# A greedy order's table of positions: rows of their own for the first and the last image, and new numbers in every row

## The chip, the cores and the metric

The kernel runs on one core of one Trainium2 chip. The metric is the device time of one execution in microseconds; of the kernel before, three runs gave 2142.4, 2146.23 and 2150.11, median 2146.23.

## The reference

The input x is 16 images of 256 channels and 56 x 56 points, float32. Two blocks follow each other, each added to its input:

```python
x = x + conv(_gn(x))        # _gn: group norm, 32 groups of 8 channels
x = x + attention(_gn(x))
```

`conv` takes the sign of its input, convolves it with weights of which only the sign and one scale per channel count (3 x 3, four groups of 64 channels, dilations 1, 3 and 5), puts each of the three results through a leaky rectifier with its own slope, sums them and normalizes over the channels. `attention` makes q, k and v of 64 channels (8 heads of 8), forms for each point the nine neighbours' scores out of q times k (a fixed and a learned depthwise part, folded into one small matrix here), takes the softmax over the nine, sums the nine values and projects back to 256 channels.

## The kernel before, in words

**Tiles.** Each image is cut into two strips (u = 0 and 1), each of four pieces of seven rows; a tile of a strip is 128 partitions x 784 points (two halves of 392). One image takes these stages, for each strip u:

- `stats`, `norm0`, `sign`: load x by channel group (`load_half`, L468), sums on ACT (L489), group norm's shift, sign into the padded bf16 image `sgn` (L514), of which there is one per channel group, and an exchange of border rows (L526, L527).
- `conv{u}`: twelve steps, channel group g by dilation d (`conv`, L554): 36 matmuls (L564) into one PSUM buffer, then ACT (L583, for d = 0, and L596) and DVE (L590, for d = 1 and 2, and L602) sum the three results in a buffer `ct`.
- `load{u}` loads x once more into `xt` (L1148). `mean{u}`, `var{u}`, `root{u}`, `scale{u}` normalize the four ct of the strip (`channel_norm`, L641: matmuls L613 and L631, DVE L660 and L689, ACT L667) and add them to xt (L703, on POOL), with the squares of the sum on ACT (L710).
- `fold`, once per image after both strips: the second group norm is folded into the weights of q, k and v (`fold`, L722; POOL L732, PE L755).
- `qkv{u}`: 16 matmuls each for q, k and v (L794), evicted by ACT (L812).
- `prod{u}`: nine products of q and a shifted k (L850); `term{u}`: ten groups of matmuls that sum them into scores (L872), in two PSUM buffers for the whole strip; `soft{u}`: transposes and the softmax (L886 to L908, on DVE, ACT and POOL).
- `value{u}`: ten groups of matmuls (L922), each evicted by a DVE product with a shifted v (L934) into a buffer `m` and summed (L948); `proj{u}`: four projections (L968) that DVE adds to xt (L979); then the store (L989).

**Buffers.** PSUM is four buffers of two banks (`ps`). There are seven `ct`, three `xh`, three `xt`, three `p` and three `m`. A strip holds its xt from the load to the store.

**What sets the order.** The kernel schedules by hand. Every step is registered with `plan.at(stage, b, i)` (L186) and an operation on an engine with a cost in us, the buffers it needs and what it reads and writes. `Plan.emit` (L223) then simulates the five engines with those costs and writes each engine's instructions in the order that it finds. In each round it takes, per engine, the operation that can start first; among those whose starts lie within AHEAD it takes the one of the lowest position, `2 * b + ORDER[stage][i]`. So 2 in the table is one image, a step at −20 goes before nearly everything, and one at 95 goes when nothing else can. Buffers of xh, xt, ct, p and m are given out in program order alone: a step that must open such a buffer waits for the earlier ones, whatever its position. HOP (0.25 us) is the planner's price of a dependency between engines.

`either` (L413) leaves products, the sum of the values and the addition to xt to POOL or DVE: DVE may take one only when it would end it more than LEAN (61.83 us) before POOL, or, for the products and sums of the last image, when LAST (−32.05) is added to its end in place of LEAN.

**The table.** ORDER has, for each stage, a row for the first image (name with `^`), one for the images between (plain) and one for the last (`$`). Before the change the three rows of a stage hold the same numbers:

```python
"term0^": (-17.28, 5.04, -6.13, -15.6, 8.43, 19.29, 31.53, 24.74, -8.75, 0.82),
"term0": (-17.28, 5.04, -6.13, -15.6, 8.43, 19.29, 31.53, 24.74, -8.75, 0.82),
"term0$": (-17.28, 5.04, -6.13, -15.6, 8.43, 19.29, 31.53, 24.74, -8.75, 0.82),
```

The order of the program (before the planner) is: weights and the first image's signs, then for each image b both strips' convolutions and channel norms, the signs of image b + 1, the fold of b, q, k and v of both strips, scores and values of strip 0, then of strip 1.

Of the kernel before, what the change touches and what calls it, by code (L numbers as in the profile page):

```python
# [68 lines left out]
class Op:  # L69
# [6 lines left out]


ORDER = {
    "first^": (24.59,),
    "second^": (30.61,),  # L80
    "start^": (-0.44, 12.01, 8.32, -11.9),
    "weights^": (16.57, 0.74, 15.54, 8.13, -15.35, 9.81),
    "stats": (-23.02, -11.03, 24.25, 43.57),
    "stats$": (-23.02, -11.03, 24.25, 43.57),
    "norm0": (-20.32,),
    "norm0$": (-20.32,),
    "sign": (-8.81, 4.11, 13.27, 36.85),
    "sign$": (-8.81, 4.11, 13.27, 36.85),
    "conv0^": (-17.27, 2.29, 28.55, -15.99, 8.45, 8.78, -5.4, 6.78, 31.53, -11.69, 14.22, 14.25),
    "conv0": (-17.27, 2.29, 28.55, -15.99, 8.45, 8.78, -5.4, 6.78, 31.53, -11.69, 14.22, 14.25),  # L90
    "conv0$": (-17.27, 2.29, 28.55, -15.99, 8.45, 8.78, -5.4, 6.78, 31.53, -11.69, 14.22, 14.25),
    "conv1^": (7.4, 12.95, 95.96, 12.79, 1.59, 12.9, 4.7, 39.18, 55.69, -8.93, 9.19, 30.54),
    "conv1": (7.4, 12.95, 95.96, 12.79, 1.59, 12.9, 4.7, 39.18, 55.69, -8.93, 9.19, 30.54),
    "conv1$": (7.4, 12.95, 95.96, 12.79, 1.59, 12.9, 4.7, 39.18, 55.69, -8.93, 9.19, 30.54),
    "load0^": (95.98,),
    "load0": (95.98,),
    "load0$": (95.98,),
    "load1^": (5.24,),
    "load1": (5.24,),
    "load1$": (5.24,),  # L100
    "mean0^": (8.83,),
    "mean0": (8.83,),
    "mean0$": (8.83,),
    "mean1^": (29.44,),
    "mean1": (29.44,),
    "mean1$": (29.44,),
    "var0^": (8.78, 11.01, 15.97, 29.02),
    "var0": (8.78, 11.01, 15.97, 29.02),
    "var0$": (8.78, 11.01, 15.97, 29.02),
    "var1^": (-9.01, 16.63, 18.58, 16.63),  # L110
    "var1": (-9.01, 16.63, 18.58, 16.63),
    "var1$": (-9.01, 16.63, 18.58, 16.63),
    "root0^": (-10.53,),
    "root0": (-10.53,),
    "root0$": (-10.53,),
    "root1^": (-17.05,),
    "root1": (-17.05,),
    "root1$": (-17.05,),
    "scale0^": (15.67, 15.06, -3, 40.43),
    "scale0": (15.67, 15.06, -3, 40.43),  # L120
    "scale0$": (15.67, 15.06, -3, 40.43),
    "scale1^": (-16.84, 17.23, 8.22, 8.83),
    "scale1": (-16.84, 17.23, 8.22, 8.83),
    "scale1$": (-16.84, 17.23, 8.22, 8.83),
    "fold^": (-12.89,),
    "fold": (-12.89,),
    "fold$": (-12.89,),
    "qkv0^": (6.66, -12.93, 15),
    "qkv0": (6.66, -12.93, 15),
    "qkv0$": (6.66, -12.93, 15),  # L130
    "qkv1^": (8.11, -17.4, 96.15),
    "qkv1": (8.11, -17.4, 96.15),
    "qkv1$": (8.11, -17.4, 96.15),
    "prod0^": (9.09, 30.51, 9.14, -13.48, 29.6, 14.43, 17.51, -16.64, -13.31),
    "prod0": (9.09, 30.51, 9.14, -13.48, 29.6, 14.43, 17.51, -16.64, -13.31),
    "prod0$": (9.09, 30.51, 9.14, -13.48, 29.6, 14.43, 17.51, -16.64, -13.31),
    "prod1^": (-14.1, 12.39, 13.44, 5.73, 7.96, 13.89, -14.32, -16.31, -9.81),
    "prod1": (-14.1, 12.39, 13.44, 5.73, 7.96, 13.89, -14.32, -16.31, -9.81),
    "prod1$": (-14.1, 12.39, 13.44, 5.73, 7.96, 13.89, -14.32, -16.31, -9.81),
    "term0^": (-17.28, 5.04, -6.13, -15.6, 8.43, 19.29, 31.53, 24.74, -8.75, 0.82),  # L140
    "term0": (-17.28, 5.04, -6.13, -15.6, 8.43, 19.29, 31.53, 24.74, -8.75, 0.82),
    "term0$": (-17.28, 5.04, -6.13, -15.6, 8.43, 19.29, 31.53, 24.74, -8.75, 0.82),
    "term1^": (-16.84, 29.94, 29.34, 11.93, 6.96, 8.07, -9.43, 13.66, 9.05, 6.97),
    "term1": (-16.84, 29.94, 29.34, 11.93, 6.96, 8.07, -9.43, 13.66, 9.05, 6.97),
    "term1$": (-16.84, 29.94, 29.34, 11.93, 6.96, 8.07, -9.43, 13.66, 9.05, 6.97),
    "soft0^": (-14.93,),
    "soft0": (-14.93,),
    "soft0$": (-14.93,),
    "soft1^": (7.31,),
    "soft1": (7.31,),  # L150
    "soft1$": (7.31,),
    "value0^": (-13.35, -23.05, -1.34, 4.34, -6.07, 9.15, -16.95, -21.09, -15.61, 39.19),
    "value0": (-13.35, -23.05, -1.34, 4.34, -6.07, 9.15, -16.95, -21.09, -15.61, 39.19),
    "value0$": (-13.35, -23.05, -1.34, 4.34, -6.07, 9.15, -16.95, -21.09, -15.61, 39.19),
    "value1^": (-19.04, 4.84, -9.61, -12.73, 6.92, 7.45, 12.47, 8.08, 28.72, 39.07),
    "value1": (-19.04, 4.84, -9.61, -12.73, 6.92, 7.45, 12.47, 8.08, 28.72, 39.07),
    "value1$": (-19.04, 4.84, -9.61, -12.73, 6.92, 7.45, 12.47, 8.08, 28.72, 39.07),
    "proj0^": (-0.81, 7.32, -11.88, -8.96),
    "proj0": (-0.81, 7.32, -11.88, -8.96),
    "proj0$": (-0.81, 7.32, -11.88, -8.96),  # L160
    "proj1^": (15.51, -16.48, -1.88, 6.47),
    "proj1": (15.51, -16.48, -1.88, 6.47),
    "proj1$": (15.51, -16.48, -1.88, 6.47),
}


class Plan:
# [5 lines left out]


    HOP = 0.25
    LEAN = 61.83
    LAST = -32.05
    AHEAD = 0.29

    def __init__(self, kinds, last):  # L180
        self.kinds, self.ops, self.wrote, self.read = kinds, [], {}, {}
# [10 lines left out]
    def op(self, eng, cost, emit, r=(), w=(), port=False, hold=(), late=0.0, other=None, lean=None):  # L192
# [6 lines left out]
        o = Op(engines, self.prio, emit, bufs, port, late)  # L199
        o.lean = self.LEAN if lean is None else lean  # L200
        for b in bufs:
# [21 lines left out]
    def emit(self):  # L223
# [4 lines left out]
        while ready:  # L228
            short, best = set(), {}
            for x in ready:  # L230
# [18 lines left out]
                for e, cost in o.engines:  # L249
# [3 lines left out]
                    elif start + cost + o.lean > done:  # L253
                        continue
                    if e not in best or start < best[e][0] - self.AHEAD:
                        best[e] = (start, x, e, cost)
# [35 lines left out]
def preact_conv_attention(  # L292
# [120 lines left out]
    def either(costs, f, r, w, b):  # L413


        engines = {"POOL": nc.gpsimd, "DVE": nc.vector}
        op("POOL", costs[0], lambda e: f(engines[e]), r, w, port=True, other=("DVE", costs[1]), lean=Plan.LAST if b == NB - 1 else None)

# [879 lines left out]
```

## Time and profile before

| what | value |
|---|---|
| runs, median (lowest to highest) | 2146.23 us (2142.4 to 2150.11) |
| the profiled execution | 2151.76 us, span 2150.0 us |
| TensorE clock granted, mean | 0.953 of full |
| instructions | 70814 |
| HBM read, written | 154.91 MB, 51.38 MB |
| first weight scaling of the fold (L732), image 0 | 155.8 us |
| the same, image 15 | 2049.1 us |

How to read what follows: an engine's busy time is that of its own instructions; a group "out<-in" names what an instruction writes and reads; "<-X" at the end of a line names what ended the idle time ahead of it. A count "x36" of L564 is one convolution step. PE is TensorE, DVE VectorE, ACT ScalarE, POOL GpSimd, and SP issues the transfers. The scaling of the weights at L732 marks the fold, so the distance from one to the next is the period of the images.

### The profile page before, as it was taken

The page shows a single profiled execution, that of the slowest core. Times are in us where ns is not written, and L with a number is a line of the kernel's source. Part 1 is how long each engine was busy: PE and PEld are TensorE (multiplying, and loading weights), DVE is VectorE, ACT ScalarE, POOL GpSimd, SP SyncE. Part 2 cuts the span into 40 slices and gives each one's busy share as a digit, 9 for nine tenths or more (in the row PEclk, how much of TensorE's full clock was granted, in tenths as well). Part 3 has the DMA queues.
Part 4 walks back from the last instruction along what each step waited for, and adds up shares of the span by engine and source line. Part 5 has one row for each costly group of instructions (what it writes and reads, how often), then busy time and mean ns, then how long its engine had stood idle before and what let it go on. Part 6 is the DMA issues. An engine that isn't in the chain of part 4 may idle for free.

```text
span 2150.0 us, 70814 instructions
## 1 busy us (share of the span) xinstructions
PE 1794.7 (83%) x31770; PEld 885.7 (41%) x31770; DVE 1711.5 (80%) x2336; ACT 1187.0 (55%) x1573; POOL 1270.2 (59%) x757
## 2 busy tenths in 40 slices
PE   5779798888989888898888888888888988889674
PEld 4444353434435343444434344343434434343231
DVE  7776968789696887969698796968969697896756
ACT  7784656556465655646575555657555555453220
POOL 2127657485675748567474855748486574847723
PEclk9889999999999999999999999999999999999787
DMA  8922635535363463446446344544544455041212
GB/s 210 192 63 54 135 81 119 128 80 119 84 140 79 111 137 80 108 96 134 85 111 130 79 105 100 133 93 111 116 87 109 95 125 108 7 101 24 61 31 61
DMA packets 102416, 216.26 MB, mean 101 GB/s; under 512 B 10721, under 2 KB 84833, under 8 KB 102113
## 3 DMA queue, kind: packets, MB, share of 16 engines
q1 hardware_dynamic: 102112, 211.74, 44.7%
q8 instruction: 249, 4.08, 0.8%
q14 instruction: 55, 0.44, 0.1%
HBM read 154.91 MB, written 51.38 MB: 96 GB/s over the span
## 4 chain that ended last, share of the span: by engine, by line
PE 39%; DVE 37%; POOL 7%; issue 6%; DMA 5%; ACT 5%; SPq 2%; DVEq 0%; POOLq 0%; ACTq 0%
PE banks L794 11%; PE banks L872 10%; DVE m L934 10%; PE banks L564 9%; DVE ct L602 8%; POOL p L850 5%; DVE ct L590 5%; PE banks L922 3%; DMA out<-xt 3%; DVE xt L979 3%; PE banks L613 2%; ACT banks L596 2%; DVE ct L660 2%; PE banks L968 1%; DVE at L908 1%
## 5 line engine op out<-in xcount | busy, mean ns | idle before, releaser
L564 PE MATMUL banks<-sgn,wconv 64*64 64x392 bf16 x13824 | 683.6, 343 | 86.5 <-DVE m L934 37.3
L850 POOL TENSOR_TENSOR p<-qt,kt 128x784 f32<-128x784 f32 x274 | 463.9, 1733 | 299.1 <-ACT qt L812 187.5
L948 POOL TENSOR_TENSOR m<-m 128x784 f32<-128x784 f32 x248 | 473.8, 1910 | 232.3 <-DVE m L934 225.7
L564 PEld LDWEIGHTS <-wconv 64*64 64x64 bf16 x13824 | 433.9, 108 | 377.2 <-issue 195.6
L596 ACT ACTIVATE banks<-banks,cbi,csc 128x784 f32<-128x784 f32 x384 | 372.2, 974 | 283.3 <-DVE ct L590 255.4
L602 DVE SCALAR_TENSOR_TENSOR ct<-banks,oalpha,ct 128x784 f32<-128x784 f32 x384 | 391.1, 1027 | 81.2 <-ACT banks L596 72.8
L590 DVE SCALAR_TENSOR_TENSOR ct<-banks,asc,ct 128x784 f32<-128x784 f32 x256 | 259.3, 1023 | 174.9 <-PE banks L564 171.1
L703 POOL TENSOR_TENSOR xt<-xt,ct 128x784 f32<-128x784 f32 x128 | 235.8, 1859 | 215.1 <-DVE ct L689 88.3
L922 PE MATMUL banks<-at,wv 64*32 64x392 f32 x5120 | 289.7, 529 | 60.6 <-DVE at L908 31.5
L934 DVE TENSOR_TENSOR m<-banks,vt 128x784 f32<-128x784 f32 x288 | 276.0, 966 | 44.2 <-PE banks L922 42.6
L872 PE MATMUL banks<-p,wk 32*64 32x392 f32 x4608 | 247.2, 518 | 67.3 <-POOL p L850 67.0
L794 PE MATMUL banks<-xt,wf 64*64 64x392 f32 x3072 | 269.1, 496 | 5.9 <-DVE ct L602 3.0
L489 ACT ACTIVATE junk<-xh 128x1568 bf16<-128x1568 f32 x124 | 186.9, 1507 | 100.9 <-DMA xh<-in_x 99.5
L710 ACT ACTIVATE junk<-xt,pr 128x784 bf16<-128x784 f32 x128 | 121.3, 948 | 104.2 <-POOL xt L703 100.9
L667 ACT ACTIVATE sq<-ct 128x784 f32<-128x784 f32 x128 | 107.8, 855 | 117.7 <-DVE ct L660 94.1
L794 PEld LDWEIGHTS banks<-xt,wf 64*64 64x64 f32 x3072 | 113.3, 134 | 141.1 <-issue 123.1
L872 PEld LDWEIGHTS banks<-p,wk 32*64 32x64 f32 x4608 | 82.8, 133 | 197.6 <-POOL p L850 135.9
L922 PEld LDWEIGHTS banks<-at,wv 64*32 64x32 f32 x5120 | 67.9, 110 | 223.0 <-issue 117.1
L514 ACT ACTIVATE sgn<-xh,g 128x1568 bf16<-128x1568 f32 x64 | 105.7, 1651 | 69.9 <-PE banks L564 67.9
L660 DVE SCALAR_TENSOR_TENSOR ct<-ct,mv,banks 128x784 f32<-128x784 f32 x128 | 124.5, 1024 | 23.3 <-PE banks L631 23.3
L968 PE MATMUL banks<-m,wp 64*64 64x392 f32 x1024 | 114.8, 551 | 28.5 <-DVE m L956 28.5
L979 DVE SCALAR_TENSOR_TENSOR xt<-banks,prb,xt 128x784 f32<-128x784 f32 x128 | 128.1, 1027 | 8.4 <-PE banks L968 7.7
(103 smaller groups left out, 1535.5 us busy)
## 6 DMA issues: line engine op xcount, KB each, us to landing
xh<-in_x SPq DMA_DIRECT2D x248, 392.0 KB, 5.5
xt<-in_x SPq DMA_DIRECT2D x128, 392.0 KB, 7.9
out<-xt SPq DMA_DIRECT2D x128, 392.0 KB, 5.7
sgn<-sgn SPq DMA_DIRECT2D x128, 41.2 KB, 4.3
p<-in_w SPq DMA_DIRECT2D x12, 144.0 KB, 5.9
wq<-in_wqkv SPq DMA_DIRECT2D x1, 384.0 KB, 6.0
cst<-in_consts SPq DMA_DIRECT2D x1, 336.0 KB, 2.9
wk<-in_wk_a SPq DMA_DIRECT2D x1, 320.0 KB, 6.7
```

The lines of the kernel that those rows point to most:

```text
L564: nc.tensor.matmul(out=ps[q * GC : (q + 1) * GC, h, 0:SN], lhsT=wconv[h * GC : (h + 1) * GC, g, d, tap, :], rhs=sgn[g][h * GC : (h + 1) * ...
L590: lambda: nc.vector.scalar_tensor_tensor(ct.tile, n(), asc[:, g, s], ct.tile, ALU.mult, ALU.add),
L596: lambda: nc.scalar.activation(n(), n(), AF.Relu, bias=cbi[:, g, s], scale=csc[:, g, s]),
L602: lambda: nc.vector.scalar_tensor_tensor(ct.tile, n(), oalpha[:, g, s], ct.tile, ALU.mult, ALU.add),
L703: lambda e, g=g: e.tensor_tensor(xt[:, g], xt[:, g], ct[g].tile, ALU.add),
L794: nc.tensor.matmul(out=ps[h * D : (h + 1) * D, q, 0:SN], lhsT=wf[q * GC : (q + 1) * GC, g, j, :], rhs=xt[q * GC : (q + 1) * GC, g, h, :], ...
L850: e.tensor_tensor(p.tile.rearrange("p x (r w) -> p x r w", w=W), _view(qt[:, 0, u * SN :], [(NU * SN + LANES, 2), (W, SR), (1, W)]), shift ...
L872: nc.tensor.matmul(out=ps[rt // 2][q * 64 : (q + 1) * 64, rt % 2, 0:n], lhsT=wk[r, j, :], rhs=rhs, start=s == 0, stop=s == 9,)
L922: nc.tensor.matmul(out=ps[rt * 32 : (rt + 1) * 32, q, 0:SN], lhsT=wv[q * 64 : (q + 1) * 64, j, :], rhs=at[q * 64 : (q + 1) * 64, rt, 0:SN] ...
L934: lambda j=j, m=m, ps=ps: nc.vector.tensor_tensor(m.tile.rearrange("p x (r w) -> p x r w", w=W), _view(ps[:, 0, :], [(512, 2), (W, SR), (1 ...
L948: lambda e, m=m, acc=acc: e.tensor_tensor(acc.tile, acc.tile, m.tile, ALU.add),
L979: lambda g=g, ps=ps: nc.vector.scalar_tensor_tensor(xt[:, g], ps[:, :, 0:SN], prb[:, g : g + 1], xt[:, g], ALU.add, ALU.add),
```

## The change

Only the table and three constants of the planner differ; no instruction is added or taken away, and the planner's code is the same. Each stage now has three different rows, and all numbers are new. The core of the diff, with the rows that the prediction speaks of:

```diff
-    "stats": (-23.02, -11.03, 24.25, 43.57),
+    "stats": (5.05, 8.05, 87.49, 4.28),
-    "conv0": (-17.27, 2.29, 28.55, -15.99, 8.45, 8.78, -5.4, 6.78, 31.53, -11.69, 14.22, 14.25),
-    "conv0$": (-17.27, 2.29, 28.55, -15.99, 8.45, 8.78, -5.4, 6.78, 31.53, -11.69, 14.22, 14.25),
+    "conv0": (-20.26, 1.17, 94.9, 4, 11.28, 19.93, -16.11, 15.26, 35.34, -25.95, 8.58, 39.23),
+    "conv0$": (2.84, 4.38, 16.27, -18.69, 6.27, 85.75, 5.77, 37.95, 88, -14.22, 4.65, 42.64),
-    "conv1": (7.4, 12.95, 95.96, 12.79, 1.59, 12.9, 4.7, 39.18, 55.69, -8.93, 9.19, 30.54),
+    "conv1": (5.6, 10.35, 107.2, 16.81, 10.91, 33.18, 18.41, 40.59, 89.85, -19.73, 34.57, 35.61),
-    "load1": (5.24,),
+    "load1": (-8.9,),
-    "scale0": (15.67, 15.06, -3, 40.43),
+    "scale0": (38.96, 13.49, 11.71, 0.28),
-    "prod0": (9.09, 30.51, 9.14, -13.48, 29.6, 14.43, 17.51, -16.64, -13.31),
+    "prod0": (8.38, -1.99, -27.48, 3.78, -18.31, 2.44, -20.69, 102.4, 17.96),
-    "term0": (-17.28, 5.04, -6.13, -15.6, 8.43, 19.29, 31.53, 24.74, -8.75, 0.82),
+    "term0": (38.71, 4.2, 1.75, -3.06, 0.48, 8.92, -21.97, 8.62, 8.11, 3.68),
-    "value0": (-13.35, -23.05, -1.34, 4.34, -6.07, 9.15, -16.95, -21.09, -15.61, 39.19),
+    "value0": (4.21, -22.06, -16.06, 6.5, 8.84, -1.21, -17.16, 4.99, 5.82, 39.12),
-    "proj0": (-0.81, 7.32, -11.88, -8.96),
+    "proj0": (-17.92, -21.81, 8.1, 6.51),
...
-    LEAN = 61.83
-    LAST = -32.05
-    AHEAD = 0.29
+    LEAN = 58.15
+    LAST = -52.33
+    AHEAD = 0.25
```

## The prediction

> **What bounds the kernel now.** I read the page first, for the shares of the engines, then the busy times by stretches, then the waits inside one image, then the timelines of the queues. No engine is full:
>
> ```profile
> PE 1794.7 (83%) x31770; PEld 885.7 (41%) x31770; DVE 1711.5 (80%) x2336; ACT 1187.0 (55%) x1573; POOL 1270.2 (59%) x757
> PE 39%; DVE 37%; POOL 7%; issue 6%; DMA 5%; ACT 5%; SPq 2%; DVEq 0%; POOLq 0%; ACTq 0%
> ```
>
> The chain that ended last is shared by PE and DVE: order and waits bound this kernel, not one engine. To see the period I use the scaling of the attention weights (POOL, L732), which happens once per image, at the fold. The timeline of POOL has, for two neighbouring images and for the last:
>
> ```profile
> 663.47 1.88 POOL L732 TENSOR_SCALAR wf<-wq,g 128x192 f32<-128x192 f32 x4 [6.43 <-DVE g L738]
> ...
> 789.79 1.88 POOL L732 TENSOR_SCALAR wf<-wq,g 128x192 f32<-128x192 f32 x4 [6.41 <-DVE g L738]
> ...
> 2049.12 1.88 POOL L732 TENSOR_SCALAR wf<-wq,g 128x192 f32<-128x192 f32 x4 [6.42 <-DVE g L738]
> ```
>
> The first of all starts at 155.8. So the span is 155.8 (ramp) + 1893.3 (15 periods, 126.2 each) + 100.9 (end) = 2150.0. The busy times by stretches (length, then PE, PEld, DVE, ACT, POOL, clock, DMA share, GB/s) show one period in pieces, then the whole of it, then the two stretches at the end:
>
> ```profile
> 675.00:695.00 20.00, 18.99 (x352) 8.94 (x352) 7.02 (x8) 8.64 (x13) 15.41 (x10) 1.00 0.30 57
> 695.00:715.00 20.00, 16.81 (x292) 6.43 (x283) 17.49 (x25) 10.26 (x13) 16.27 (x10) 0.91 0.38 87
> 715.00:751.30 36.30, 29.84 (x554) 13.54 (x547) 33.15 (x44) 28.32 (x37) 26.94 (x15) 0.95 0.52 117
> 751.30:789.80 38.50, 32.39 (x644) 18.95 (x646) 36.40 (x55) 20.52 (x31) 20.42 (x12) 1.00 0.54 119
> 663.50:789.80 126.30, 109.32 (x1974) 53.98 (x1969) 102.41 (x139) 74.00 (x99) 80.89 (x49) 0.97 0.49 107
> 2015.20:2049.10 33.90, 14.81 (x170) 5.84 (x166) 23.34 (x37) 8.77 (x16) 19.40 (x11) 0.74 0.59 129
> 2049.10:2150.00 100.90, 64.44 (x904) 22.75 (x904) 64.87 (x68) 8.45 (x12) 29.59 (x18) 0.82 0.17 38
> ```
>
> In 675 to 695 PE is full and DVE idles 13 of 20 us; from 715 on it is DVE that is full. Neither is kept busy through the period: PE idles 17.0 us, DVE 23.9. Why can't the next image slide in? The queue of transfers has the answer, a loop with little slack:
>
> ```profile
> 751.28 4.74 SPq L989 DMA_DIRECT2D out<-xt  x4
> 760.89 3.23 SPq L1148 DMA_DIRECT2D xt<-in_x  x4
> ```
>
> xt has three buffers, so strip 1 of the next image loads only when strip 0 of this one has been stored. Fold at 663.5, store at 751.3 (87.8 us), load issued at 760.9 once the store has landed; the last part lands at 771.4; the additions (L703) run from 775.0 to 783.4; fold at 789.8. The load is ready 3.6 us before its first use. So the loop is 87.8 + 20.1 + 3.6 + 8.4 + 6.4 = 126.3, the period.
>
> [...] PE stands still for POOL's product (L872 behind L850, 4.2 us in this period) with later matmuls written behind it. So the order that the planner writes down is the order that runs, and a wrong guess stalls its engine. [...] at 2026.97 a DVE operation (L681) takes 1.88 us where its mean is 0.41, beside POOL's addition. The planner counts this only for the operations marked for it.
>
> **The change part by part.** No instruction is added or removed by the diff. What moves is the order of 16 images' steps, and by LAST and LEAN the choice between POOL and DVE for products and additions. All of that changes at once, so I price it by stage, with the few positions that can be read.
>
> *LEAN 61.83 to 58.15, AHEAD 0.29 to 0.25.* In the groups, POOL has 274 of 288 products and 248 of 256 additions; DVE has 14 and 8, all in the last image. A backlog of 58 us on POOL doesn't occur at 81 us of work in 126. Cost 0. If it did, each product moved would be 1.06 us on DVE instead of 1.73 on POOL. AHEAD moves choices between starts 0.25 to 0.29 us apart: 0.
>
> *LAST −32.05 to −52.33.* Both allow DVE in the last image unless it ends over 32 (or 52) us after POOL, and no such backlog is in the 100.9 us of the end. Cost 0, at most one addition (0.97 us) either way.
>
> *The middle images (14 periods).* Read the loop: of the 87.8 us from fold to store, strip 0's own chain needs less. In the last image, where only strip 1 competes, the fold is at 2049.1 and the store at 2121.9: 72.8 us. So 15.0 us of it is work of the next image, queued in front. If a new order kept all of that out of the way, the loop alone would allow 126.3 − 15.0 − 3.6 = 107.7, below PE's 109.3; if PE idled nowhere, 17.0 us per period would be won. Those are upper ends. Two positions can be read. Statistics (L489 on ACT, 8 x (1.51 + 0.19) = 13.6 us per image) went first, at −23.02 and −11.03; they go to 5.05, 8.05 and 87.49, behind ACT's evictions. What DVE waits for them is inside L602 behind L596, 4.4 us in this period: worth 0 to 4.4. Against it, the opening of strip 0's scores (term0, its first step) goes from −17.28 to 38.71, so that convolutions of the next image (conv1, from 5.6 + 2 on) may pass it. That feeds the DVE that idles at 675 to 695 (13 us), but each convolution put ahead costs the loop 1.74 us of PE. Values and projections keep their rank: value0's last step is 39.19, then 39.12, and the rest still stands mostly ahead of conv1. I take an eighth of the 15.0 us: 1.8 us per period, 14 x 1.8 = 25 us. Nothing in the trace fixes this share; both ends (a gain of 5 per period and a loss of 4) go into the range. What is late next is DVE, which from 695 on has 87.0 of 94.8 us busy: its 102.4 us per period and PE's 109.3 stay.
>
> *The transfers of these steps (SP).* The loads for the statistics (L468) move with them, and load1 goes from 5.24 to −8.9. SP issues in order and waits in its queue: its timeline has eight of L468 from 723.9 to 739.7, 15.8 us for buffers of xh, with everything later behind them. The store at 751.28 follows the last L979 (751.25) at once, so such a wait costs nothing now. Should one fall ahead of the store or of the load of xt, it would cost the loop up to 15.8 less 3.6; should the load go out sooner, nothing is won, since it waits for the store. I take 0.
>
> *The end.* conv0$ opens at 2.84 where conv0 opens at −20.26, and ct's buffers are taken in that order, so image 14's attention goes further ahead of image 15's convolutions. Now about 15 of image 15's 24 convolutions are done by the fold of image 14, and then 2015 to 2049 has nothing to run: PE 14.8 of 33.9 us, while the loop (store, load, additions, squares, fold) is waited for. The store at 2015.2 is 86.5 after the fold at 1928.7; at 72.8 it would be 13.7 earlier. I take 8 of that, and bound it by 0 and 13.7. In the last 100.9 us PE and DVE each have 64 busy; the rest is dependence between two strips. Better interleaving may give 0 to 10; I take 3.
>
> *The ramp.* The first convolution starts at 33.3. Until then 220 GB/s are moved, a DMA bound that order hardly changes. From 33.3 to 155.8 PE has 93.2 and DVE 93.8 of 122.5, with 15 convolutions of image 1 inside (15 x 1.78 = 27 us of PE). Putting image 0 strictly first brings its fold forward, but what is displaced returns in the next period. Net 2, between −4 and 10.
>
> Sum: 25 + 8 + 3 + 2 = 38 us. The profiled execution took 2151.8 (its span and 1.8 around it), so 2114 by it; the median of the runs is 5.5 lower, and 2146.2 − 38 = 2108.
>
> **The rivals.** *Ends only*: the loop keeps its 126.3, because strip 0's chain is filled again with other work, and only end and ramp gain: 13 to 15 us, 2132. For it: the 3.6 us of slack, and ranks that stay in the values. Against: 17 us of PE idle per period. *No effect*: the ends' holes are the loop's own latency, and what is won in the ramp comes back: 2146. *Slower, the opening of the scores*: term0's first step at 38.71 lets convolutions go ahead until the ct buffers are gone. Seven buffers less strip 0's four leave nine convolutions of strip 1, three to four of which are done by the fold. With four put ahead, 4 x 1.74 = 7.0 us of delay go to the store; 3.6 is slack, 3.4 is period: 14 x 3.4 = 47 us, 2194 without the 13 of the ends, 2181 with them. It decides from the third convolution ahead of L872's first matmul.
>
> **How the numbers follow.** What can be told from no change is 0.3%, 6.4 us. Middle and ends gain: 0.43, at 2070 to 2125. Ends only: 0.28, at 2120 to 2139. No effect: 0.09. Slower: 0.20, at 2153 to 2200. That makes faster 0.71, same 0.09, slower 0.20. The likeliest is 2108. For 8 in 10 I go from 2068, below which a gain of over 4 us per period would be needed, to 2165, which takes in the lower half of the slower case.
>
> **What would show it.** Right: L732 every 124 to 125 us; L989's first store under 86 us after it; DVE over 9 us busy in the 20 us after qkv; PE over 18 in the stretch before the last fold. Ends only: L732 still every 126. Wrong by the rival: three or more groups of L564 between L794 and L872, and the store over 91 us after the fold. If PE's busy time per image grows, or the clock falls, the cause is none of mine.

## The result and the profile after

| | before | after |
|---|---|---|
| runs, median (lowest to highest) | 2147.2 us (2142.13 to 2150.11, 8 runs) | 2137.51 us (2135.4 to 2140.39, 8 runs) |
| ratio, 95% interval | | 0.9959 (0.9946 to 0.9972) |
| profiled execution, span | 2151.76 us, 2150.0 us | 2138.15 us, 2136.4 us |
| first fold (L732), image 0 | 155.8 us | 146.8 us |
| fold of image 2, of image 12 | 410.7, 1674.7 us | 409.4, 1672.3 us |
| mean period between them | 126.40 us | 126.29 us |
| fold of image 15 | 2049.1 us | 2036.2 us |
| TensorE clock granted, mean of the profiled execution | 0.953 | 0.944 |

The change makes the kernel 0.41% faster, 9.7 us between the medians, where 38 were forecast. The page's shares first. They show as little as before: PE 11 us busier, DVE 2 less, and no engine full.

```profile
PE 1806.0 (85%) x31770; PEld 893.0 (42%) x31770; DVE 1709.7 (80%) x2337; ACT 1186.1 (56%) x1573; POOL 1265.0 (59%) x756
PE 46%; DVE 25%; POOL 11%; issue 10%; ACT 4%; DMA 3%; SPq 0%; POOLq 0%; DVEq 0%; ACTq 0%
```

The counts of POOL and DVE differ by one from those before. By line it is three operations of the last image: two sums of values (L948, POOL 246 in place of 248) went to DVE and one product (L850, POOL 275 in place of 274) to POOL. More than that LEAN, LAST and AHEAD did not move between the engines. POOL's timeline gives the folds of image 0, of two neighbours and of image 15:

```profile
146.84 1.87 POOL L732 TENSOR_SCALAR wf<-wq,g 128x192 f32<-128x192 f32 x4 [8.79 <-DVE g L738]
...
661.94 1.87 POOL L732 TENSOR_SCALAR wf<-wq,g 128x192 f32<-128x192 f32 x4 [6.53 <-DVE g L738]
788.24 1.87 POOL L732 TENSOR_SCALAR wf<-wq,g 128x192 f32<-128x192 f32 x4 [6.54 <-DVE g L738]
...
2036.21 1.87 POOL L732 TENSOR_SCALAR wf<-wq,g 128x192 f32<-128x192 f32 x4 [3.86 <-DVE g L738]
```

The difference of one fold to the next tells where the time went. Image 0 folds 9.0 us sooner, but the next two periods take 134.2 and 128.4 in place of 128.5 and 126.4, and at the fold of image 2 only 1.3 us are left. The ten periods from there to image 12 take 1262.9 in place of 1264.0: 1.1 us, a tenth of a microsecond each. The last three periods take 363.9 in place of 374.4 (10.5, from the printed folds), and what follows the last fold 100.2 in place of 100.9. That is all of the 13.6 us between the spans.

The stretches of one period, of the period as a whole and of the two at the end (columns as in the prediction: length, PE, PEld, DVE, ACT, POOL, clock, DMA share, GB/s):

```profile
673.40:693.40 20.00, 19.55 (x358) 9.10 (x356) 7.21 (x8) 7.03 (x10) 15.60 (x10) 1.00 0.17 38
693.40:713.40 20.00, 17.47 (x308) 6.40 (x300) 17.96 (x25) 10.21 (x13) 16.60 (x11) 0.91 0.38 87
713.40:748.50 35.10, 28.25 (x550) 13.50 (x535) 33.70 (x45) 28.88 (x37) 28.18 (x15) 1.00 0.53 121
748.50:788.20 39.70, 34.10 (x626) 19.13 (x629) 36.50 (x53) 19.22 (x29) 18.52 (x10) 0.91 0.55 121
661.90:788.20 126.30, 110.87 (x1976) 54.47 (x1968) 102.72 (x139) 73.99 (x99) 80.76 (x48) 0.96 0.49 107
2004.60:2036.20 31.60, 16.75 (x253) 6.42 (x230) 25.92 (x39) 9.38 (x19) 22.08 (x12) 0.81 0.51 110
2036.20:2136.40 100.20, 64.17 (x904) 22.03 (x904) 64.08 (x69) 8.33 (x12) 26.19 (x17) 0.81 0.20 47
```

Line by line they are close to those of before. In the 20 us from 673.4 on, around the end of q, k and v, PE is full and DVE busy for 7.21 us, as it was for 7.02. The period's account on DVE reads 102.7 busy + 23.6 idle; before it was 102.4 + 23.9. All positions are new, and still DVE's idle time is nearly the same. The timelines say why. PE's, before:

```profile
673.20 8.13 PE L794 MATMUL banks<-xt,wf 64*64 64x392 f32 x96
681.15 1.73 PE L564 MATMUL banks<-sgn,wconv 64*64 64x392 bf16 x36
682.81 0.95 PE L872 MATMUL banks<-qt,wk 32*64 32x416 f32 x16
```

and after:

```profile
668.78 10.76 PE L794 MATMUL banks<-xt,wf 64*64 64x392 f32 x128
679.36 1.73 PE L564 MATMUL banks<-sgn,wconv 64*64 64x392 bf16 x36
681.02 0.95 PE L872 MATMUL banks<-qt,wk 32*64 32x416 f32 x16
```

A block of sums for q, k and v, then one convolution, then the scores: the new numbers wrote the same sequence at the place where DVE starves. Behind the fold's own matmuls (L755) the block even has a fourth group in a row; before, two of the five groups stood ahead of them and three behind, now it is one and four. DVE's timeline has the wait that this makes, the first operation after the block, before:

```profile
682.93 1.03 DVE L590 SCALAR_TENSOR_TENSOR ct<-banks,asc,ct 128x784 f32<-128x784 f32 x1 [8.68 <-PE banks L564]
```

and after:

```profile
681.14 1.03 DVE L590 SCALAR_TENSOR_TENSOR ct<-banks,asc,ct 128x784 f32<-128x784 f32 x1 [9.52 <-PE banks L564]
```

The queue of transfers shows the store of strip 0 at 86.5 us after the fold, where it was 87.8, and the load of xt behind it:

```profile
748.46 4.75 SPq L989 DMA_DIRECT2D out<-xt  x4
758.07 3.09 SPq L1148 DMA_DIRECT2D xt<-in_x  x4
```

The load has landed at 768.2. The additions that use it begin at 773.0. So 1.3 us were won up to the store, and the slack behind the load grew by about as much, from 3.6 to 4.8. POOL's timeline names what the additions wait for, after:

```profile
773.03 3.67 POOL L703 TENSOR_TENSOR xt<-xt,ct 128x784 f32<-128x784 f32 x2 [9.75 <-DVE ct L689]
```

and before:

```profile
774.96 3.68 POOL L703 TENSOR_TENSOR xt<-xt,ct 128x784 f32<-128x784 f32 x2 [5.16 <-DVE ct L689]
```

Both times it is DVE's product with the scale (L689), not the transfer. This line stood in the trace before the prediction was made, and the loop over xt that the prediction put together runs across it.

### The profile page after: what moved, and what is told of

Its sections match the earlier page's. It is cut to its first block, busy times and chain, and to the rows that moved or that the text cites. A ratio compares the mean times of both kernels' runs of the same rounds, so it can differ in the third digit from the quotient of the medians.

```text
span 2136.4 us, 70807 instructions
## 1 busy us (share of the span) xinstructions
PE 1806.0 (85%) x31770; PEld 893.0 (42%) x31770; DVE 1709.7 (80%) x2337; ACT 1186.1 (56%) x1573; POOL 1265.0 (59%) x756
## 4 chain that ended last, share of the span: by engine, by line
PE 46%; DVE 25%; POOL 11%; issue 10%; ACT 4%; DMA 3%; SPq 0%; POOLq 0%; DVEq 0%; ACTq 0%
PE banks L564 15%; PE banks L794 12%; PE banks L872 8%; DVE ct L602 7%; POOL p L850 6%; DVE m L934 5%; POOL m L948 4%; DVE ct L590 4%; PE banks L968 3%; PE banks L922 3%; PE banks L613 3%; DMA xh<-in_x 2%; ACT banks L596 2%; DVE ct L660 1%; DVE xt L979 1%
## 5 line engine op out<-in xcount | busy, mean ns | idle before, releaser
L850 POOL TENSOR_TENSOR p<-qt,kt 128x784 f32<-128x784 f32 x275 | 465.4, 1727 | 289.1 <-ACT qt L812 175.7
L948 POOL TENSOR_TENSOR m<-m 128x784 f32<-128x784 f32 x246 | 469.2, 1908 | 195.9 <-DVE m L934 188.9
L596 ACT ACTIVATE banks<-banks,cbi,csc 128x784 f32<-128x784 f32 x384 | 373.6, 975 | 266.7 <-DVE ct L590 249.9
L602 DVE SCALAR_TENSOR_TENSOR ct<-banks,oalpha,ct 128x784 f32<-128x784 f32 x384 | 390.4, 1027 | 82.5 <-ACT banks L596 82.0
L590 DVE SCALAR_TENSOR_TENSOR ct<-banks,asc,ct 128x784 f32<-128x784 f32 x256 | 261.0, 1024 | 205.2 <-PE banks L564 199.4
L922 PE MATMUL banks<-at,wv 64*32 64x392 f32 x5120 | 281.8, 513 | 65.2 <-DVE m L934 32.5
L872 PE MATMUL banks<-p,wk 32*64 32x392 f32 x4608 | 254.6, 533 | 48.6 <-POOL p L850 47.3
L667 ACT ACTIVATE sq<-ct 128x784 f32<-128x784 f32 x128 | 109.7, 858 | 117.3 <-DVE ct L660 81.1
L794 PEld LDWEIGHTS banks<-xt,wf 64*64 64x64 f32 x3072 | 116.4, 134 | 134.2 <-issue 117.8
L872 PEld LDWEIGHTS banks<-p,wk 32*64 32x64 f32 x4608 | 84.1, 135 | 178.3 <-POOL p L850 105.0
L968 PE MATMUL banks<-m,wp 64*64 64x392 f32 x1024 | 128.4, 608 | 29.2 <-DVE m L956 27.2
L583 ACT ACTIVATE ct<-banks,asc 128x784 f32<-128x784 f32 x128 | 116.5, 910 | 57.1 <-PE banks L564 56.0
```

The lines of the kernel that those rows point to most:

```text
L590: lambda: nc.vector.scalar_tensor_tensor(ct.tile, n(), asc[:, g, s], ct.tile, ALU.mult, ALU.add),
L596: lambda: nc.scalar.activation(n(), n(), AF.Relu, bias=cbi[:, g, s], scale=csc[:, g, s]),
L602: lambda: nc.vector.scalar_tensor_tensor(ct.tile, n(), oalpha[:, g, s], ct.tile, ALU.mult, ALU.add),
L794: nc.tensor.matmul(out=ps[h * D : (h + 1) * D, q, 0:SN], lhsT=wf[q * GC : (q + 1) * GC, g, j, :], rhs=xt[q * GC : (q + 1) * GC, g, h, :], ...
L850: e.tensor_tensor(p.tile.rearrange("p x (r w) -> p x r w", w=W), _view(qt[:, 0, u * SN :], [(NU * SN + LANES, 2), (W, SR), (1, W)]), shift ...
L872: nc.tensor.matmul(out=ps[rt // 2][q * 64 : (q + 1) * 64, rt % 2, 0:n], lhsT=wk[r, j, :], rhs=rhs, start=s == 0, stop=s == 9,)
```

## The experiments

Three explanations compete for the missing gain in the middle. **Stretches** (S): the period is a stretch after the fold in which PE is full and DVE starves, and then one in which DVE is full; only work taken from the engine that is full in its stretch shortens it. **Loop** (L): store and load of xt close the period, as the prediction had it. **Clock** (C): the new order does gain, and TensorE's half-clock windows take it back. Four runs ahead of those ask whether the three sets of rows can be told apart at all.

**The rows of the middle alone.** The changed kernel, with the numbers of each plain row in its rows for the first and the last image too:

```diff
-    "conv0$": (2.84, 4.38, 16.27, -18.69, 6.27, 85.75, 5.77, 37.95, 88, -14.22, 4.65, 42.64),
+    "conv0$": (-20.26, 1.17, 94.9, 4, 11.28, 19.93, -16.11, 15.26, 35.34, -25.95, 8.58, 39.23),
...
```

> The changed kernel with the new middle rows in all three places, so that the first and the last image have no rows of their own; constants as changed. Theory A (the gain sits in the last image's rows alone, the middle is worth nothing, the first image's gain is handed back): steady period 126.3 us, no gain over the kernel before, 2140 to 2155 us. Theory B (the new middle gains, and the profile of one execution hid it): under 2140 us, period under 126.

Measured: 2160.76 us (2157.45 to 2166.7), 1.0054 of before (1.0037 to 1.0072). Its folds are at 160.1, 1679.2 and 2049.9 us (images 0, 12, 15), with 126.3 from image 7 on. So the new middle (with the new constants) in the place of the old one is slower, by more than either expectation allowed for: it loses 4.3 us in the ramp and 7.6 behind the last fold. From image 0 to image 12 it brings nothing (1519.1 us, before 1518.9), and between the folds of images 12 and 15 it wins 3.7 (370.7 in place of 374.4).

**Without the rows of the first image, and without those of the last.** The same edit for the names with `^` alone, and for those with `$` alone.

> The changed kernel without the first image's own rows (the middle rows stand in for them). Theory A: the fold of image 0 comes 9 us or more later than the changed kernel's 146.8, but most of it comes back in the next two periods (134.2 and 128.4 there), so the whole is within 5 us of the changed kernel, 2135 to 2143. Theory B (the first image's rows are worth what the ramp shows): 2146 to 2155.

> The changed kernel without the last image's own rows. Theory A: all of the end's gain goes: the last two periods are 124 to 127 and 118 to 121 in place of 120.2 and 117.1, the stretch after the last fold is longer than 100.2, and the whole is 8 to 14 us longer than the changed kernel, 2145 to 2152. Theory B (the gain is in the middle or the ramp): within 3 us of 2137.5.

Measured: 2148.25 us without the first (1.0002 of before, 0.9993 to 1.0011), 2151.95 without the last (1.0017, 1.0008 to 1.0025). POOL's timeline without the first image's rows has image 0 and image 12 at

```profile
161.44 1.86 POOL L732 TENSOR_SCALAR wf<-wq,g 128x192 f32<-128x192 f32 x4 [7.54 <-DVE g L738]
...
1680.84 1.87 POOL L732 TENSOR_SCALAR wf<-wq,g 128x192 f32<-128x192 f32 x4 [6.18 <-DVE g L738]
```

that is 8.6 us behind the changed kernel at image 12. Beside the new middle, then, the first image's rows are worth 10.7 us of time (2148.25 − 2137.51) and the last image's 14.4. Against the old kernel they bring far less, because a part of them repairs what the new middle would cost at the ends: the ramp that it would lengthen to 161.4, and the 108.7 us behind the last fold in the run without the last rows (span 2149.2):

```profile
2040.48 1.86 POOL L732 TENSOR_SCALAR wf<-wq,g 128x192 f32<-128x192 f32 x4 [5.35 <-DVE g L738]
```

Of the 10.5 us won between the folds of images 12 and 15, 5.9 are there without the rows of the last image (368.5 in place of 374.4), and 4.6 come with them: part of what was won at the end comes from the new middle.

**The new ends beside the old middle.** The kernel before, with its plain rows and constants, and the changed kernel's rows for the first and last image.

```diff
-    "conv0$": (-17.27, 2.29, 28.55, -15.99, 8.45, 8.78, -5.4, 6.78, 31.53, -11.69, 14.22, 14.25),
+    "conv0$": (2.84, 4.38, 16.27, -18.69, 6.27, 85.75, 5.77, 37.95, 88, -14.22, 4.65, 42.64),
...
```

> The kernel before with the changed kernel's rows for the first and the last image, the middle rows and the constants as before. If rows can be judged one by one: near the changed kernel, 2133 to 2145, since the middle seems worth nothing. If rows are a matched set (the first image's order decides in what phase the middle's order starts): the first few periods are far from 126, over 140 us, and the whole is over 2190.

Measured: 2253.29 us, 1.0484 of before (1.0465 to 1.0502). The first four periods are 155.6, 159.2, 144.4 and 148.4, then 124.5 to 127.4. None of the four partial sets is as fast as the whole one, and this one is much slower. So what a part "is worth" holds only beside the others.

**Four edits of work, the order kept (S against L).** Each leaves some arithmetic out of the changed kernel (its expectation says which) and leaves the plan alone, so that the order of everything else stays. Each was executed once, so the periods within its trace say more than its time. They take away PE's work at q, k and v; PE's work in convolutions of strip 0; DVE's work in strip 0's convolutions; DVE's work in strip 1's convolutions just after the fold (the lines below show one of this last edit's two places; it leaves out two of L590 as well).

```diff
-            for g in range(NG):
+            n = NG // 2 if j == 0 or (j == 2 and u == 0) else NG
+            for g in range(n):
...
-            for tap in range(9):
+            taps = 6 if u == 0 and 3 * g + d in (0, 1, 3, 4, 5, 6, 7) else 9
+            for tap in range(taps):
...
+        skip = u == 0 and 3 * g + d in (0, 3, 4, 6)
-            lambda: nc.vector.scalar_tensor_tensor(ct.tile, n(), oalpha[:, g, s], ct.tile, ALU.mult, ALU.add),
+            lambda: skip
+            or nc.vector.scalar_tensor_tensor(ct.tile, n(), oalpha[:, g, s], ct.tile, ALU.mult, ALU.add),
...
+        skip = u == 1 and 3 * g + d in (5, 6, 7)
```

> The changed kernel with its order kept, leaving out half of the sums over channels (8 of 16 matmuls) of q of both strips and of v of strip 0: 24 matmuls of L794 per image less, some 4.0 us of PE, all in the stretch after the fold in which PE is full and DVE idles. Theory S (the period is a stretch bound by PE and then one bound by DVE, one after the other): period shorter by 3 to 4 us, 122.3 to 123.3. Theory L (the loop over the store and the reload of xt sets it, as the prediction said): the same sign, since this chain is in the loop too, so the run must be read with f2 to f4. Theory N (no single stretch; PE's sum counts): 3 to 4 us as well.

> The changed kernel with its order kept, leaving out three of nine taps of seven of strip 0's twelve convolution steps: 84 matmuls of L564 per image less, some 4.0 us of PE, nearly all in the stretch in which DVE is full. Theory S: nothing, period 125.8 to 126.3. Theory N (PE's sum counts): 122.3 to 123.3.

> The changed kernel with its order kept, leaving out four of the twelve L602 of strip 0 (the rectified part of four convolution steps), 3.8 us of DVE per image, in the stretch in which DVE is full. Theory S: period shorter by 3 to 4 us, 122.3 to 123.3. Theory L: the same only as far as these stood ahead of strip 0's last values. Theory N: nothing.

> The changed kernel with its order kept, leaving out five DVE operations of strip 1's convolution steps 5, 6 and 7 (three L602, two L590), 4.8 us of DVE per image, in the stretch right after the fold, in which DVE idles 15 us. Theory S: nothing, period 125.8 to 126.3. If DVE's sum counts: 121.5 to 122.5.

| left out, per image | time | period |
|---|---|---|
| 4 us of PE at q, k and v | 2086.22 us | 123.1 mean, 122.9 late |
| 4 us of PE in strip 0's convolutions | 2142.45 us | 126.3 (125.9, 126.8, 126.2 in turn) |
| 3.8 us of DVE in strip 0's convolutions | 2122.95 us | 124.5 (123.5 and 125.6 in turn) |
| 4.8 us of DVE just after the fold | 2138.21 us | 126.3 |

The same 4 us of PE give 3.3 us of period in one place and nothing to speak of in the other. Stretches of one period, with less PE at q, k and v:

```profile
773.70:896.70 123.00, 106.84 (x1924) 52.08 (x1920) 102.72 (x138) 73.86 (x99) 80.65 (x48) 0.96 0.50 109
```

with less PE in the convolutions, three periods:

```profile
1041.50:1420.30 378.80, 324.51 (x5656) 153.45 (x5652) 307.83 (x414) 221.53 (x295) 242.11 (x144) 0.95 0.49 107
```

with less DVE in strip 0's convolutions, two periods:

```profile
1035.80:1284.90 249.10, 219.10 (x3941) 106.71 (x3936) 198.97 (x269) 147.80 (x197) 161.49 (x97) 0.97 0.49 108
```

and with less DVE just after the fold:

```profile
788.40:914.70 126.30, 110.86 (x1975) 54.09 (x1971) 97.76 (x134) 74.01 (x99) 80.76 (x49) 0.96 0.49 107
```

Read DVE's busy time against the length. In the first the busy time is unchanged (102.72) and the idle time falls from 23.6 to 20.3: that is the period's gain. In the last DVE has 5 us less to do, and all of it becomes idle time. DVE's timeline of the first shows the place, the wait behind the block of q, k and v, 5.57 in place of 9.52:

```profile
665.65 1.03 DVE L590 SCALAR_TENSOR_TENSOR ct<-banks,asc,ct 128x784 f32<-128x784 f32 x1 [5.57 <-PE banks L564]
```

S holds for three of the four; of the DVE work taken from the full stretch only half, 1.8 of 3.8 us, came out as time (the part on the clock returns to this). L isn't told apart by the first of them, since strip 0's way to its store begins with the same sums.

**A fourth buffer for xt (L).** The load no longer needs the store just ahead of it; the planner plans with four.

```diff
-    kind("xt", [P, NG, 2, SN], 3)
+    kind("xt", [P, NG, 2, SN], 4)
```

> The changed kernel with four buffers of xt in place of three (rows as changed, planned anew), so that strip 1's load waits for no store. Theory L (the loop that the prediction named sets the period): 119 to 125. Theories C and S: the load was 4.8 us early as it was, so 126.3 stays.

Measured: 2138.6 us in one execution, every period from image 2 to 12 at 126.3. Counted from the start of the run to 756 us, this kernel has issued

```profile
L1148 SPq DMA_DIRECT2D xt<-in_x x48: 595/618/1395, 42.0 to 666.0; - x48
L703 POOL TENSOR_TENSOR xt<-xt,ct x44: 1841/1858/1895, 98.0 to 737.0; 128x784 f32<-128x784 f32 x44
```

48 parts of loads against 44 additions, where the changed kernel has 44 and 44: the data of the strip that is added next was asked for by 666.0. Its additions still begin at

```profile
773.57 3.66 POOL L703 TENSOR_TENSOR xt<-xt,ct 128x784 f32<-128x784 f32 x2 [9.75 <-DVE ct L689]
```

so the transfer comes some 100 us ahead, and the period is the same to a tenth. L falls.

**The clock (C).** In the changed kernel's trace every change of the granted clock lies on a fixed grid of 3.413 us, to within 0.004 us, and the clock is full or half, nothing else; one step of the grid is called a window here. Of the 71 windows in which PE was busy for less than half, 65 are followed by one at half the clock, and of the other 553 only 4 are; in the kernel before it is 50 of 65, and 9 of the other 563. Two neighbouring windows of the changed kernel, the first with PE busy for 1.68 of 3.41 us, the second at half the clock:

```profile
757.86:761.27 3.41, 1.68 (x32) 0.44 (x25) 3.41 (x5) 2.46 (x3) 2.66 (x2) 1.00 0.55 131
761.27:764.69 3.42, 3.36 (x40) 2.02 (x43) 2.99 (x5) 0.87 (x2) 1.86 (x1) 0.51 1.03 213
```

and two convolutions on PE's timeline, one of them in the second window:

```profile
752.52 1.74 PE L564 MATMUL banks<-sgn,wconv 64*64 64x392 bf16 x36
...
761.33 3.15 PE L564 MATMUL banks<-sgn,wconv 64*64 64x392 bf16 x36 [0.40 <-DVE m L934]
```

Each period of the changed kernel has three windows at half clock, at 44.8, 99.4 and 109.7 us after the fold; before there were mostly two, at 47 and 67. Several steady periods are whole multiples of the grid: 126.29 is 37.0 of it, 122.9 (less PE at q, k and v) 36.0, two periods of 249.1 (less DVE) 73.0. So it could be that the new order is shorter and waits for the grid. Five kernels fill the gaps with matmuls that repeat or aren't used: values of strip 1 twice; those and half a sum for v once more; those values with 32 short matmuls among the scores; and two with more of them.

```diff
-                for rt in range(4):
+                for _ in range(2 if u == 1 and j >= 7 else 1):
+                    for rt in range(4):
...
-            for g in range(NG):
+            for n in (NG // 2, NG) if j == 2 and u == 1 else (NG,):
+                for g in range(n):
...
+                if u == 1 and s == 4:
+                    for _ in range(4):
+                        for q in range(2):
+                            for rt in range(4):
...
+                for _ in range((2, 2, 3)[j - 7] if u == 1 and j >= 7 else 2 if u == 0 and j in (7, 8) else 1):
```

> The changed kernel with its order kept; the matmuls of strip 1's last three values (L922, steps 7 to 9) are issued twice, with the same result. 24 matmuls more per image, 2.5 us of PE, placed where PE idles ahead of the stretches of half clock at 99.4 and 109.7 us after the fold. Theory C (the period hangs on the clock: a low activity window takes the next 3.41 us at half clock, that holds the chain to the fold back by 1 us, and the period locks to 37 windows, 126.3): these two low windows go, and the period falls to 124.5 to 125.6 in spite of more work; 2120 to 2130 us. Theory S alone (a stretch of PE, then one of DVE, no part for the clock): 126.3 to 127.5.

> As g1, and half of the sum of v of strip 1 (8 matmuls of L794, 1.4 us of PE) is computed once more ahead of the whole of it, to fill the wait of the scores for POOL ahead of the low window at 44.8. Theory C: as g1 or up to 0.5 shorter, if strip 1's scores are on the chain; 124.3 to 125.6. Theory S alone: 127 to 129, since the stretch in which PE is full grows.

> The changed kernel with its order kept and matmuls without use placed where PE idles ahead of all three low windows of a period: those of strip 1's values 7 and 8 twice and 9 three times (same result), and 32 short ones (96 columns, into columns of the scores' buffers that nothing reads) after step 4 of strip 1's scores, where PE waits 2.4 us for POOL. Some 5 us of PE more per image. Theory C (low activity windows cost the middle images what the new order had saved): at most one low window per period is left, and the period is 124.3 to 125.7, or a lock at some other multiple of 3.41 us between two and three periods; 2118 to 2132 us. Theory S alone (PE's work counts where it is full, the clock doesn't matter): 126.3 or more.

> The changed kernel with the extra matmuls of the run h1_filled (values 7 to 9 of strip 1 issued two, two and three times, 32 short unused matmuls after the fifth scores step of strip 1) and with steps 7 and 8 of strip 0's values (L922) issued twice, about 63 to 66 us after the fold, where PE was busy under half of a clock window and the window after it was granted half the clock. If a half-clock window near 67 us is what made two of three periods in h1_filled 126.7 to 127.0 in place of 125.3, all periods become 125.2 to 125.5, L732 falls on no multiple of 3.413 us, and the time goes to 2140.5 - 14 x 1.0 = 2126 (2120 to 2131). If the half clock is only a companion of the longer periods, and something else holds the mean, it stays at 126.3 to 126.5 and the time at 2137 to 2143, although the window near 67 is gone. If the doubled values delay strip 0 (each holds a PSUM buffer 0.8 us longer), 2145 to 2160.

> As i1_filled_early, with 64 short unused matmuls in place of 32 after the fifth scores step, to fill the wait for POOL's products 42 to 45 us after the fold as well, so that the half-clock window near 46 us goes too. If the half clock takes time from the period, 124.5 to 125.3 and 2113 to 2126. If it does not, 126.3 to 126.5 and 2137 to 2143. If the extra 0.6 us stands in the way of strip 0's values behind it, a little more than i1_filled_early.

| filled | time, ratio to before | mean clock | half-clock windows in a period | periods |
|---|---|---|---|---|
| values of strip 1 | 2141.33 us, 0.9962 (0.995 to 0.9975) | 0.955 | 2 | 125.7, 126.7, 126.6 in turn |
| and half a sum of v | 2184.34 us, 1.0156 (1.0136 to 1.0177) | 0.948 | 3 | 129.7 |
| values, 32 short | 2140.5 us, 0.9951 (0.9934 to 0.9967) | 0.960 | 1 or 2 | 125.3, 126.9, 126.8 in turn |
| also values of strip 0 | 2146.39 us, 0.9995 (0.9982 to 1.0008) | 0.972 | 0 or 1 | mean 126.8 |
| and 64 short | 2145.83 us, 0.9995 (0.9985 to 1.0005) | 0.976 | 0 in most | 126.0, and 127.5 three times |

In the last of these kernels most periods have no half-clock window. One of them:

```profile
916.50:1042.50 126.00, 112.34 (x2200) 57.21 (x2192) 103.14 (x139) 74.06 (x99) 80.94 (x48) 1.00 0.49 107
```

That is 126.0 with the clock at 1.00, against 126.3 at 0.96. It doesn't show that the half clock costs nothing, since the fill has a price of its own. In this period DVE waits less for convolutions (11.2 us in place of 12.9 ahead of L590), but more for the doubled values and the scores (3.1 + 0.9 us in place of 2.1 + 0.5), and is 0.4 us busier. What the clock gives, the added matmuls take again. They lengthen the last two periods too (125.0 and 119.8, 120.2 and 117.1 without them).

The price of the half clock shows without a fill in two of the runs above. With the rows of the middle alone, and without those of the first image, the middle images have the changed kernel's order on all of PE, DVE, ACT and POOL. In each of the two runs one period, from image 4 to image 5, has a single half-clock window, 45 us after the fold, and takes 124.5 us; the later ones up to image 13 have two and take 126.2 to 126.3. With the rows of the middle alone:

```profile
670.80:795.30 124.50, 108.01 (x1976) 54.08 (x1968) 102.67 (x138) 74.23 (x99) 80.82 (x48) 0.99 0.50 108
1174.10:1300.40 126.30, 109.68 (x1976) 54.81 (x1972) 102.62 (x139) 74.19 (x99) 80.82 (x49) 0.97 0.49 106
```

DVE is as busy in both, and waits 1.8 us less in the first. One such wait stands in the changed kernel behind the convolution of 3.15 us:

```profile
766.84 1.03 DVE L590 SCALAR_TENSOR_TENSOR ct<-banks,asc,ct 128x784 f32<-128x784 f32 x1 [1.27 <-PE banks L564]
```

and the same operation in the period of 124.5 has:

```profile
774.53 1.03 DVE L590 SCALAR_TENSOR_TENSOR ct<-banks,asc,ct 128x784 f32<-128x784 f32 x1 [0.22 <-PE banks L564]
```

So the half-clock windows behind the one at 45 us cost some 1.8 us per period. But the old order pays for them as well. The new ends beside the old middle give a period with the old order and a single such window, 45 us after the fold:

```profile
760.70:885.20 124.50, 107.85 (x1975) 53.35 (x1970) 102.51 (x139) 74.14 (x99) 80.73 (x49) 0.99 0.50 108
```

With two windows, at 47 and 67, the new order takes 126.2 to 126.3 in these runs and the kernel before 126.3 to 126.8. With equal windows, then, the two orders take nearly the same time, and C falls as the explanation of 25 us: the clock lengthens the periods of both, and takes back no gain of that size from the new one. This rests on few periods. Three of the old order with the single window at about 46.6 us took 125.2, so that up to 0.7 us per period (10 us in 14) between the orders isn't excluded.

It also answers S's open half. With less DVE in strip 0's convolutions the periods of 123.5 have two half-clock windows, those of 125.6 three: 2.8 us were won in the first, 0.7 in the second. With 32 short matmuls the periods of 125.2 to 125.3 have one window and those of 126.6 to 127.4 two. With less PE in the convolutions two of three periods have four windows and the third has three; that one takes 126.2, so the added windows hide no gain of 3 us there. It isn't the number alone: with the values of strip 1 twice all periods have two, and the short ones are those in which the two aren't neighbours. After a period of 124.5, which is 36.5 times the grid, the next image meets the windows 1.8 us later (the first at 46.7 after the fold, not 44.9) and has two of them again; at 126.3, 37.0 times the grid, it stays so. From these figures I estimate that a gain of a microsecond or so may fail to show in a period that keeps step with the grid. No run stayed at 124.5. Nor was a full clock seen without added work. The second kernel, meant to lose about its added 1.4 us, lost 3.4 per period and came to 38.0 of the grid.

**A little more on DVE's chain.** One short operation of strip 1's norm (L679, 0.3 us) is issued twice:

```diff
+        def plus():
+            for _ in range(1 + u):
+                nc.vector.tensor_scalar(v.tile, var(), EPS_LN, None, ALU.add)
```

> The changed kernel with its order kept and one small DVE operation more per image (L679 of strip 1 twice, with the same result), 0.3 us, in the middle of the chain from the last convolution to the fold, in the stretch in which DVE is full. Theory C: the lock to 37 windows takes it up, period 126.3 as before. Theory S alone: 126.6.

Measured: 2155.93 us in the one execution, 127.5 in the mean of the periods from image 2 to 12, which neither expectation had. The single periods lie between 125.7 and 130.3 and follow the half-clock windows: with two 125.7 to 125.8, with three 126.8 to 127.5, with four 128.5, with five 130.2. So the 1.2 us per image aren't the price of 0.3 us of DVE alone, and no cost of an operation can be read from them.

## Why the prediction was wrong in size

The direction was right, and the measured time lies where the recorded rival "Ends only" put it (2132; measured 2137.5). The rival's reason, the loop that keeps its 126.3, isn't what held the period. By the terms of the sum:

- **The middle, 25 us: the step that failed.** It measured 1.1 us over the ten periods from image 2 to 12, 0.1 us each in place of 1.8. "I take an eighth of the 15.0 us: 1.8 us per period" assumed two things. The first is that a shorter way from fold to store shortens the period. The store did come 1.3 us earlier, some two thirds of the 1.8, and it became slack behind the load. The step "the loop is 87.8 + 20.1 + 3.6 + 8.4 + 6.4 = 126.3" adds up a slack as if it were a part of the loop. A chain with slack in it isn't the one that binds; the additions waited for L689, as POOL's line shows, and with four buffers the period is unchanged. The second is that new positions would feed DVE in the 20 us after q, k and v. "DVE over 9 us busy" was the sign; it is 7.21. Single periods of the new middle did take 124.5, within the forecast's 124 to 125, but by their half-clock windows, and the old middle has one as well.
- **"What is late next is DVE"** was closer than the loop. From 693 on DVE has 88.2 of 94.8 us busy after the change, as it had 87.0 of 94.8 before. The two stretches, PE's and DVE's, were both in the prediction's first view. The runs with work left out, and the one with four buffers, show that they, and not the transfer, make the period.
- **The clock**, no term in the sum for the middle: the recorded sign, "if PE's busy time per image grows, or the clock falls, the cause is none of mine", came about. PE has 110.9 us in place of 109.3 in the period, and the clock 0.96 in place of 0.97, by a third half-clock window. The third costs nothing that shows (126.3 with three, 126.3 with two). Against a single one, two or three cost up to 1.8 us per period, before as after. That 14 times this is again 25 us is chance.
- **The statistics, 0 to 4.4 us for DVE's wait** inside L602 behind L596: this wait is 4.9 us in the period after. It gained nothing.
- **The opening of the scores**, the rival "Slower": from three convolutions ahead of L872 on it would cost. There is one, as before, so its condition never came about, although the opening's number went from −17.28 to 38.71. The number alone doesn't tell the place; what can start at that moment does.
- **The transfers, 0:** the eight loads of L468 stand in SP's queue from 720.7 to 735.2, and the next store is at 748.5. Right.
- **LEAN, LAST, AHEAD, 0:** three operations changed their engine, all in the last image; DVE has one more of them than before. What that alone was worth wasn't run.
- **The end, 8 + 3 us:** 10.5 + 0.7. Right in sum, and placed otherwise. Most was won one period sooner, between the folds of images 13 and 14 (126.3 to 120.2), where the prediction had looked at the stretch before the last fold; there PE has 16.75 of 31.6 us busy, not the 18 that was set as a sign, up from 14.8 of 33.9. The interleaving after the last fold brought 0.7 of the 3. And the last image's rows weren't the only cause: 5.9 of the 10.5 are there without them.
- **The ramp, 2 us:** 1.3 left at image 2. "What is displaced returns in the next period" is what the periods of 134.2 and 128.4 show. The DMA engines' busy share up to 33.3 us was 0.92 before, at 220 GB/s, and 0.88 after, at 215.

With 1.5 for the 14 middle periods (0.1 each) in place of 25, the same sum gives 14.5 us, 2132; the runs' medians differ by 9.7, since the profiled execution of before, 2151.76, lies 4.6 above their median. Executions of one program differ with the clock: of 39 of the kernel before, the 20 with a mean clock up to 0.955 have the median 2151.1, the 14 from 0.957 on 2143.3.

What stays open: whether an order with a convolution inside the block of q, k and v would give the 3.3 us that leaving out a part of the block gave, and whether one that keeps PE busy where the half-clock windows now arise, without added work, would stay at 124.5. No such order was run, and no version with all its work ran here that is faster than the changed kernel.

## What to carry to other kernels

Before a loop is written as a sum, look at what ended the wait at each of its joints: where a part of the sum is slack, another chain is the late one, and time won on the loop only makes the slack larger. A table of priorities says little about an order; compare the sequence at the place where the late engine starves, since there two very different tables wrote the same three lines. Rows for the first and last image are to be judged with the middle they were found with: beside another they cost 4.8%. And before two periods are compared, count their half-clock windows: the same order took 124.5 us with one and 126.3 with two.

## What the runs showed of the hardware

In the traces of both kernels PE's granted clock was full or half and changed only on a grid of 3.413 us. Of the windows with PE busy for less than half, 65 of 71 were followed by one at half the clock (before the change 50 of 65), of the others 4 of 553 (9 of 563). Behind one with PE busy for 1.68 of 3.41 us a convolution took 3.15 in place of 1.74 us. Several steady periods were 36.0, 37.0 and 38.0 times 3.413 us, or 36.5 in the mean of two that alternate; one in which no window was at half took 36.9 times as long as a window, off the grid. One order of instructions took 124.5 us with one half-clock window in the period and 126.3 with two or three: VectorE waited 1.27 us behind the convolution of 3.15 us, and 0.22 at the same place in the shorter period. Filling the gaps with useless matmuls raised the mean clock from 0.944 to as much as 0.976 and made no run shorter (2140.5 to 2184.34 us, without them 2137.51). In the period at the full clock VectorE waited 3.1 + 0.9 us for the doubled values and the scores, where it waited 2.1 + 0.5 without them.

What the planner wrote down is what ran: before the change VectorE's 2207 operations, GpSimd's 746, ScalarE's 1320 and SP's 654 transfers stand in the trace in the order in which the program issues them, line by line, and TensorE's matmuls in its 1013 groups by line; after the change likewise, with 2208, 745, 1320, 654 and 1040.
